# Layer 2's scans joined into one product, and pool waits narrowed to the bytes that are reused, in a four-layer image network

## The chip, the cores and the metric

The kernel runs on one core of one Trainium2 chip. The metric is the device time in microseconds of one execution. The kernel before takes 7064.17 us (median of 3 runs, 7053.81 to 7065.25); the profiled execution spans 7063.8 us. Everything is float32.

The engines are named as in the profile: PE is TensorE (matrix products; PEld is its loading of weights, which overlaps the products), DVE is VectorE, ACT is ScalarE, POOL is GpSimd, SP is the engine whose queue starts most DMA transfers. SBUF is the on-chip memory with 128 partitions, PSUM the smaller one in which TensorE leaves its results, and DRAM the memory outside.

## The reference

Four residual layers on x of shape 8 x 56 x 56 x 192. Each one is `x = x + layer(groupnorm(x))`:

```python
x = x + _L0(_gn(x))   # gated Toeplitz mixing along rows and columns
x = x + _L1(_gn(x))   # attention in shifted 7 x 7 windows
x = x + _L2(_gn(x))   # 3 x 3 convolution and running averages
x = x + _L3(_gn(x))   # 7 x 7 convolution, LayerNorm, wide MLP with gelu
```

The part that is rewritten lies in layer 2. It projects to 384 channels, convolves each channel, and adds running averages in four directions:

```python
def ema_scan(x, axis):                 # s = 0.6 s + 0.4 x, along one axis
    ...
proj  = jnp.einsum('bhwd,dc->bhwc', x, W_in) + b_in
local = depthwise_conv_3x3(proj)       # cut: the call
lr = ema_scan(local, 3)                # left to right
rl = flip(ema_scan(flip(local, 3), 3), 3)
tb = ema_scan(local, 2)                # top to bottom
bt = flip(ema_scan(flip(local, 2), 2), 2)
mixed = 0.25 * (lr + rl + tb + bt) + local
# then LayerNorm over the channels and W_out
```

## The kernel before

The program works through nine stages, one after the other: `qv` (layer 0, projections), `mix` (layer 0, Toeplitz products), `l1` (layer 1), `l2i`, `mx`, `l2o` (layer 2: in, mixing, out), `l3i`, `cv`, `l3o` (layer 3: in, convolution, out). Each stage opens pools of its own for SBUF and PSUM and closes them at its end; between stages the images pass through DRAM (`x1`, `x2`, `pd`, `md`, `xd`, `zd`, `yd`). A new stage's pools use the bytes of the pools that were closed:

```python
    with ExitStack() as st:
        pool = st.enter_context(tc.tile_pool(name="l2i", bufs=2))
        psum = st.enter_context(tc.tile_pool(name="l2ip", bufs=4, space=PSUM))
        w_in = resident("w_in", nc.gpsimd, pool)
        b_in = resident("b_in", nc.gpsimd, pool)
        for b in range(nimg):
            layer2_in(b, pool, psum, w_in, b_in)
    layer2_mix()
    with ExitStack() as st:
        pool = st.enter_context(tc.tile_pool(name="l2o", bufs=2))
        # ... and so on for every stage
```

Without any other word, a pool's first users wait until everything of the pool that it replaces is done. `bufs=2` gives each name in the pool two buffers. The tiles lie in the order in which their names are first used. The order of instructions in each engine's queue is fixed when the program is built; it follows the program's text, except that an instruction that is expected to be ready sooner may go ahead of one that is not.

Layer 2's mixing works on 24 groups of 16 channels, all 8 images at once. A column of 128 partitions holds two neighbouring rows of an image: row 0 of the pair on the upper 64 partitions, row 1 on the lower 64, the 56 pixels of a row reversed. `NPAIR` is 28 pairs of rows, `NG` is 8 x 28 = 224 columns of one channel. Running top to bottom over rows is then a scan over pairs with the factor 0.6 x 0.6 = 0.36, and the left and right averages within a row are part of the matrix `ema`:

```python
            for g in range(C2 // CG2):
                cs = slice(g * CG2, (g + 1) * CG2)
                wt = pool.tile([128, CG2, 256], F32, name="wt2")
                nc.sync.dma_start(wt, ...)                      # band matrices of 16 channels
                zc = pool.tile([128, nimg, CG2, P2], F32, name="zc2")
                for b in range(nimg):
                    nc.sync.dma_start(zc[:, b], pd[b][:, cs])
                loc = pool.tile([128, CG2, NG], F32, name="loc")
                fwd = pool.tile([128, CG2, NG], F32, name="fwd")
                bwd = pool.tile([128, CG2, NG], F32, name="bwd")
                for c4 in range(0, CG2, 4):
                    ps = psum.tile([128, 2, 512], F32, name="cv2")
                    for i in range(4):
                        dst = ...
                        for q in range(2):
                            nc.tensor.matmul(                   # the convolution
                                dst, wt[:, c4 + i, 128 * q:128 * q + 128], zc[:, :, c4 + i, q:q + NPAIR],
                                start=(q == 0), stop=(q == 1),
                            )
                    nc.scalar.copy(
                        loc[:, c4:c4 + 4].rearrange("p (j i) z -> p j (i z)", j=2), ps[:, :, 0:2 * NG]
                    )
                for h in range(2):
                    ...
                    nc.vector.tensor_tensor_scan(f(fwd), d, f(loc), 0.0, ALU.mult, ALU.add)
                    nc.vector.tensor_tensor_scan(
                        _reversed(f(bwd)), d, _reversed(f(loc)), 0.0, ALU.mult, ALU.add
                    )
                yc = pool.tile([2 * W, nimg, CG2, NPAIR], F32, name="yc2")
                for c4 in range(0, CG2, 4):
                    ps = psum.tile([2 * W, 2, 512], F32, name="mx2")
                    for i in range(2):
                        for k, z in enumerate((loc, fwd, bwd)):
                            nc.tensor.matmul(                   # three products, summed in PSUM
                                ps[:, i, 0:2 * NG], ema[:, k],
                                z[:, c4 + 2 * i:c4 + 2 * i + 2].rearrange("p c z -> p (c z)"),
                                start=(k == 0), stop=(k == 2),
                            )
                    for i in range(2):                          # src, dst: cut
                        if i == 0:
                            nc.vector.tensor_copy(dst, src)
                        else:
                            nc.scalar.copy(dst, src)
                for b in range(nimg):
                    nc.sync.dma_start(md[b][:, cs], yc[:, b])
```

A float32 product of this program appears in the trace as two matmul instructions.

Of the kernel before, what the change touches and what calls it, by code (L numbers as in the profile page):

```python
# [76 lines left out]
def kernel(ctx: ExitStack, tc: tile.TileContext, a: dict, out: bass.AP):  # L77
# [208 lines left out]


    def build_bias_mask(psum):
        with tc.tile_pool(name="bm", bufs=2) as pool:
            rev = pool.tile([WN, WN], F32, name="rev", bufs=1)  # L290
            nc.gpsimd.dma_start(rev, a["rev49"])

# [482 lines left out]
    def layer2_mix():  # L775

        band = a["band2"]
        with ExitStack() as st:  # L780
            pool = st.enter_context(tc.tile_pool(name="mx", bufs=2))
            psum = st.enter_context(tc.tile_pool(name="mxp", bufs=2, space=PSUM))
            ema = resident("ema", nc.gpsimd, pool)
            NG = nimg * NPAIR
            dec = pool.tile([128, CG2 * nimg, NPAIR], F32, name="dec2", bufs=1)
            nc.gpsimd.memset(dec, 0.36)
            nc.gpsimd.memset(dec[:, :, 0:1], 0.0)
            dec = dec.rearrange("p c n -> p (c n)")
            for g in range(C2 // CG2):
                cs = slice(g * CG2, (g + 1) * CG2)  # L790
                wt = pool.tile([128, CG2, 256], F32, name="wt2")
                nc.sync.dma_start(
                    wt, bass.AP(band.tensor, band.offset + g * CG2 * BL2, [[1, 128], [BL2, CG2], [1, 256]])
                )
                zc = pool.tile([128, nimg, CG2, P2], F32, name="zc2")
                for b in range(nimg):
                    nc.sync.dma_start(zc[:, b], pd[b][:, cs])
                loc = pool.tile([128, CG2, NG], F32, name="loc")
                fwd = pool.tile([128, CG2, NG], F32, name="fwd")
                bwd = pool.tile([128, CG2, NG], F32, name="bwd")  # L800
                for c4 in range(0, CG2, 4):
                    ps = psum.tile([128, 2, 512], F32, name="cv2")
                    for i in range(4):
                        dst = ps[:, i // 2, NG * (i % 2):NG * (i % 2 + 1)].rearrange("p (b n) -> p b n", n=NPAIR)
                        for q in range(2):
                            nc.tensor.matmul(  # L806
                                dst, wt[:, c4 + i, 128 * q:128 * q + 128], zc[:, :, c4 + i, q:q + NPAIR],
                                start=(q == 0), stop=(q == 1),
                            )
                    nc.scalar.copy(  # L810
                        loc[:, c4:c4 + 4].rearrange("p (j i) z -> p j (i z)", j=2), ps[:, :, 0:2 * NG]
                    )
                for h in range(2):
                    hs = slice(h * CG2 // 2, (h + 1) * CG2 // 2)
                    f = lambda z: z[:, hs].rearrange("p c z -> p (c z)")
                    d = dec[:, 0:CG2 // 2 * NG]
                    nc.vector.tensor_tensor_scan(f(fwd), d, f(loc), 0.0, ALU.mult, ALU.add)  # L817
                    nc.vector.tensor_tensor_scan(
                        _reversed(f(bwd)), d, _reversed(f(loc)), 0.0, ALU.mult, ALU.add
                    )  # L820
                yc = pool.tile([2 * W, nimg, CG2, NPAIR], F32, name="yc2")
                for c4 in range(0, CG2, 4):
                    ps = psum.tile([2 * W, 2, 512], F32, name="mx2")
                    for i in range(2):
                        for k, z in enumerate((loc, fwd, bwd)):
                            nc.tensor.matmul(  # L826
                                ps[:, i, 0:2 * NG], ema[:, k],
                                z[:, c4 + 2 * i:c4 + 2 * i + 2].rearrange("p c z -> p (c z)"),
                                start=(k == 0), stop=(k == 2),
                            )  # L830
                    for i in range(2):
                        src = ps[:, i, 0:2 * NG].rearrange("p (c b n) -> p b c n", c=2, n=NPAIR)
                        dst = yc[:, :, c4 + 2 * i:c4 + 2 * i + 2]
                        if i == 0:
                            nc.vector.tensor_copy(dst, src)
                        else:
                            nc.scalar.copy(dst, src)
                for b in range(nimg):
                    nc.sync.dma_start(md[b][:, cs], yc[:, b])

    def layer2_out(b, pool, psum, w_out):

# [76 lines left out]
    def convolve():  # L919

        band = a["band"]
        with ExitStack() as st:
            pool = st.enter_context(tc.tile_pool(name="cv", bufs=2))
            psum = st.enter_context(tc.tile_pool(name="cvp", bufs=3, space=PSUM))
            for g in range(C // CG):
                cs = slice(g * CG, g * CG + CG)
                wt = pool.tile([OP, CG, BAND], F32, name="wt")
# [95 lines left out]

    scsh = const.tile([128, nimg, 2, 3], F32, name="scsh")
    with ExitStack() as st:
        pool = st.enter_context(tc.tile_pool(name="qv", bufs=2))
        psum = st.enter_context(tc.tile_pool(name="qvp", bufs=4, space=PSUM))
        w_qv = resident("w_qv", nc.scalar, pool)
        b_qv = pool.tile([2 * W, 2, D1], F32, name="b_qv", bufs=1)
        nc.scalar.dma_start(b_qv.rearrange("p a d -> p (a d)"), a["b_qv"].partition_broadcast(2 * W))  # L1030
        tz = st.enter_context(tc.tile_pool(name="tz", bufs=2))
        x = layer0_load(0, pool)
        xn = layer0_in(0, x, pool, psum)
        blocks = toeplitz_rows(psum, tz)
        build_bias_mask(psum)
        for b in range(nimg):

            between = {i: blocks.pop(0) for i in (1, 7, 12) if blocks}
            ahead = []
            if b + 1 < nimg:  # L1040
                x = layer0_load(b + 1, pool)
                between[4] = lambda: ahead.append(layer0_in(b + 1, x, pool, psum))
            layer0_qv(b, xn, pool, psum, w_qv, b_qv, between)
            xn = ahead[0] if ahead else None
        for block in blocks:
            block()
    with ExitStack() as st:
        pool = st.enter_context(tc.tile_pool(name="mix", bufs=2))
        psum = st.enter_context(tc.tile_pool(name="mixp", bufs=2, space=PSUM))
        w_p = resident("w_p", nc.gpsimd, pool)  # L1050
        w_o = resident("w_o", nc.gpsimd, pool)

        ops = [psum.tile([128, 8, H], F32, name=f"op{k}", bufs=1) for k in range(2)]
        for op in ops:
            nc.vector.memset(op, 0.0)
        layer0_mix(pool, psum, ops, w_p, w_o)


    with ExitStack() as st:
        pool = st.enter_context(tc.tile_pool(name="l1", bufs=2))  # L1060
        psum = st.enter_context(tc.tile_pool(name="l1p", bufs=1, space=PSUM))
        consts = layer1_weights(pool, psum)

        ones2 = pool.tile([128, 128], F32, name="ones2", bufs=1)
# [46 lines left out]


    with ExitStack() as st:
        pool = st.enter_context(tc.tile_pool(name="l2i", bufs=2))
        psum = st.enter_context(tc.tile_pool(name="l2ip", bufs=4, space=PSUM))
        w_in = resident("w_in", nc.gpsimd, pool)
        b_in = resident("b_in", nc.gpsimd, pool)
        for b in range(nimg):
            layer2_in(b, pool, psum, w_in, b_in)
    layer2_mix()  # L1120
    with ExitStack() as st:
        pool = st.enter_context(tc.tile_pool(name="l2o", bufs=2))
        psum = st.enter_context(tc.tile_pool(name="l2op", bufs=2, space=PSUM))
        w_out = resident("w_out", nc.gpsimd, pool)
        for b in range(nimg):
            layer2_out(b, pool, psum, w_out)
    with ExitStack() as st:
        pool = st.enter_context(tc.tile_pool(name="l3i", bufs=2))
        psum = st.enter_context(tc.tile_pool(name="l3ip", bufs=2, space=PSUM))
        gmat = resident("gmat", nc.gpsimd, pool)  # L1130
        for b in range(nimg):
            layer3_in(b, pool, psum)


    convolve()
    with tc.tile_pool(name="l3o", bufs=2) as pool, tc.tile_pool(name="l3op", bufs=2, space=PSUM) as psum:
        w0 = resident("w0", nc.gpsimd, pool)
        w1 = resident("w1", nc.gpsimd, pool)
        dwb = pool.tile([OP, C], F32, name="dwb", bufs=1)
# [6 lines left out]
def _lay_out(inp):  # L1146
# [37 lines left out]
        band2[:, 126 + 64 * i:129 + 64 * i] = l2("conv_w")[:, 0, i]  # L1184
    at = 127 - (64 * np.arange(2)[:, None] + np.arange(W))
    eye, near = np.eye(W), 0.6 ** np.abs(np.arange(W)[:, None] - np.arange(W))
    ema = np.zeros((128, 3, 2, W))
    for r in range(2):
        for s in range(2):
            back = 0.6 ** (s - r)  # L1190
            ema[at[r], 0, s] = (1.1 * eye + 0.1 * near) if r == s else -eye / 6.0
            ema[at[r], 1, s] = 0.1 * back * eye
            ema[at[r], 2, s] = 0.1 / back * eye

    b_in = np.zeros((2, 64, 3, 2, C2), np.float32)
    b_in[:, 0:W] = l2("b_in")
# [25 lines left out]
        "w_qkv": twice(l1("w_qkv")), "w_proj": halves(l1("w_proj")), "sel": sel,  # L1222
        "rel": l1("rel_table")[::-1].T, "mask": l1("mask_matrix"),
        "w_in": twice(l2("W_in")), "b_in": b_in.reshape(128, 3, 2, C2), "band2": band2,
        "ema": ema.reshape(128, 3, 2 * W).astype(np.float32), "w_out": blocks(l2("W_out")),
        "w0": twice(l3("w0")), "w1": blocks(l3("w1")),
    }.items()}

# [17 lines left out]
```

## Time and profile before

| what | us or share |
|---|---|
| time, median of 3 | 7064.17 |
| TensorE busy | 6002.1 (85%) |
| VectorE busy | 3210.2 (45%) |
| ScalarE busy | 1811.4 (26%) |
| GpSimd busy | 1039.3 (15%) |
| DRAM traffic | 147 GB/s over the span |
| share of TensorE in the chain that ended last | 60% |
| stretch of layer 2's mixing stage | 4225 to 5050 |

The profile is one execution. A line of a group of instructions gives the source line, the engine, the operation, the tile written and the tiles read, the shapes, how many, the busy time and mean duration, and at the end the idle time of the engine before them with what ended it. A stretch gives, between two times, how long each engine was busy (with the number of instructions), the clock that TensorE was granted as a share of full speed, the share of time that the DMA engines were busy, and what they moved. Matrix products overlap in the pipeline, so their mean duration is more than the time from one to the next. A busy share over the whole span hides that stages have different limits, so the stages are looked at one by one.

### The profile page before, as it was taken

To read this page: it belongs to the slowest core of one execution; us is meant where nothing else is said; L and a number is where in the kernel's file an instruction comes from. 1 tells how busy PE (TensorE), PEld (TensorE's weight loads), DVE (VectorE), ACT (ScalarE), POOL (GpSimd) and SP (SyncE) were. 2 spreads that over 40 slices of the span, in tenths; PEclk is the share of its full clock that TensorE was granted. 3 is DMA by queue.
4 is the path that set the end of the run, shared out by engine and by line. 5 is a ranking of instruction groups with operands and counts; after the bars stand their busy time and mean duration, and the time that the engine had idled before them with its cause. 6 is when DMAs were issued, how large, how long until landed. Compare 5 with 4: busy or idle time off the path is not lost.

```text
span 7063.8 us, 126329 instructions
## 1 busy us (share of the span) xinstructions
PE 6002.1 (85%) x56258; PEld 3967.7 (56%) x56258; DVE 3210.2 (45%) x4598; ACT 1811.4 (26%) x2528; POOL 1039.3 (15%) x564
## 2 busy tenths in 40 slices
PE   6789989999999688888885878999688569698999
PEld 5568767777777344544553445666434369444444
DVE  6677733333333344444443764555477521423231
ACT  2234421111111233333331001111255100133333
POOL 4200033333333011211221000000000000101000
PEclk8889989999999788888886889999888579799999
DMA  8998886555554524444424545455577679412120
GB/s 196 210 199 173 166 287 231 222 216 216 216 216 171 77 41 57 57 56 58 57 43 76 171 157 200 165 171 174 143 170 167 182 260 325 138 50 78 52 64 25
DMA packets 1045489, 1047.05 MB, mean 148 GB/s; under 512 B 831340, under 2 KB 963860, under 8 KB 1017424
## 3 DMA queue, kind: packets, MB, share of 16 engines
q1 hardware_dynamic: 1031776, 973.57, 49.9%
q0 software_dynamic: 11440, 62.42, 3.5%
q8 instruction: 441, 7.23, 0.4%
q10 hardware_dynamic: 1728, 2.99, 0.1%
q14 instruction: 104, 0.85, 0.0%
HBM read 693.71 MB, written 345.07 MB: 147 GB/s over the span
## 4 chain that ended last, share of the span: by engine, by line
PE 60%; DVE 14%; DMA 9%; issue 6%; ACT 4%; SPq 3%; POOL 3%; DVEq 0%; another core or an unknown queue 0%; POOLq 0%; ACTq 0%
PE op L404 7%; PE qv L348 6%; PE po L1009 5%; PE pj L426 5%; PE y L447 5%; PE ph L1000 5%; PE qk_ps L627 3%; PE cps L940 3%; PE mx L826 3%; DVE ln_st L207 3%; PE cv L806 3%; PE pr L729 2%; DMA x<-x 2%; DVE fwd L817 2%; PE po L870 2%
## 5 line engine op out<-in xcount | busy, mean ns | idle before, releaser
L348 PE MATMUL qv<-w_qv_sb,xn 64*112 64x288 f32 x5376 | 733.3, 427 | 104.2 <-DVE act L354 104.2
L348 PEld LDWEIGHTS qv<-w_qv_sb,xn 64*112 64x112 f32 x5376 | 560.9, 184 | 273.8 <-DVE act L354 130.6
L385 POOL COPY lc<-lt 128x1792 f32<-128x1792 f32 x144 | 474.2, 3295 | 834.2 <-PE op L404 745.7
L404 PE MATMUL op<-rt,lc 128*56 128x56 f32 x9216 | 561.6, 275 | 3.2 <-DMA rt<-right 2.9
L404 PEld LDWEIGHTS op<-rt,lc 128*56 128x56 f32 x9216 | 507.7, 145 | 75.7 <-issue 58.8
L1009 PE MATMUL po<-hid,w_sb 128*64 128x392 f32 x2304 | 399.8, 506 | 64.7 <-ACT hid L1004 64.7
L1000 PE MATMUL ph<-y,w_sb 64*128 64x392 f32 x2304 | 423.8, 501 | 10.4 <-ACT hid L1004 10.4
L355 ACT ACTIVATE act<-act 112x576 f32<-112x576 f32 x448 | 301.1, 683 | 500.5 <-DVE act L354 499.9
L426 PE MATMUL pj<-xn,w_p_sb 64*128 64x392 f32 (+1 forms) x1920 | 372.8, 510 | 27.6 <-DVE xn L468 23.1
L447 PE MATMUL y<-pp,w_o_sb 128*64 128x392 f32 (+1 forms) x1920 | 353.1, 499 | 1.6 <-DVE pp L440 1.2
L1016 DVE TENSOR_TENSOR x<-x,z 128x392 f32<-128x392 f32 x96 | 54.5, 568 | 646.7 <-ACT z L1014 646.7
L440 DVE TENSOR_TENSOR pp<-pp,ot 128x784 f32<-128x784 f32 (+1 forms) x160 | 155.1, 969 | 404.6 <-ACT pp L431 396.8
L354 DVE TENSOR_TENSOR act<-qv,b_qv 112x576 f32<-112x576 f32 x448 | 317.2, 749 | 37.7 <-PE qv L348 37.7
L1000 PEld LDWEIGHTS ph<-y,w_sb 64*128 64x128 f32 x2304 | 233.1, 189 | 175.9 <-issue 26.7
L1009 PEld LDWEIGHTS po<-hid,w_sb 128*64 128x64 f32 x2304 | 165.3, 140 | 295.8 <-issue 225.1
L806 PE MATMUL cv<-zc,wt 128*128 128x224 f32 x1536 | 301.7, 355 | 29.8 <-DMA zc<-pd 29.8
L940 PE MATMUL cps<-zc,wt 128*128 128x224 f32 x1536 | 299.4, 356 | 30.4 <-DMA zc<-zd 28.8
L627 PE MATMUL qk_ps<-xr,wg 64*96 64x392 f32 x1536 | 311.4, 514 | 13.8 <-ACT qk L633 10.5
L806 PEld LDWEIGHTS cv<-zc,wt 128*128 128x128 f32 x1536 | 290.6, 189 | 46.2 <-issue 39.2
L940 PEld LDWEIGHTS cps<-zc,wt 128*128 128x128 f32 x1536 | 289.7, 189 | 40.0 <-issue 32.6
L764 PE MATMUL pin<-w_in_sb,xn 64*128 64x384 f32 x1392 | 259.9, 520 | 57.2 <-POOL xn L755 38.2
L431 ACT ACTIVATE pp<-pj,vecs_sb 128x784 f32<-128x784 f32 (+1 forms) x160 | 146.3, 915 | 571.3 <-PE pj L426 569.1
(220 smaller groups left out, 8873.1 us busy)
## 6 DMA issues: line engine op xcount, KB each, us to landing
lt<-left SPq DMA_DIRECT2D x72, 1792.0 KB
rt<-right SPq DMA_DIRECT2D x72, 1792.0 KB
left<-qv SPq DMA_DIRECT2D x224, 252.0 KB
right<-qv SPq DMA_DIRECT2D x448, 126.0 KB
wt<-in_band_dram SPq DMA_DIRECT2D x24, 2048.0 KB
wt<-in_band_dram SPq DMA_DIRECT2D x12, 4096.0 KB
pd<-pt SPq DMA_DIRECT2D x8, 5568.0 KB
zc<-pd SPq DMA_DIRECT2D x192, 232.0 KB
```

The source lines that it names most:

```text
L348: nc.tensor.matmul(ps[s][:, which, 0:D1 // 2], xn[64 * s:64 * s + 64, j, bass.ts(i, 2 * W)], w_qv[64 * s:64 * s + 64, j, which, ns], start ...
L354: nc.vector.tensor_tensor(act, ps[s][:, :, 0:D1 // 2], b_qv[:, :, ns], ALU.add)
L355: nc.scalar.activation(act, act, AF.Silu)
L385: nc.gpsimd.tensor_copy(lc.rearrange("p (u d) w -> p u d w", u=nu), raw[0].rearrange("p (w u d) -> p u d w", u=nu, d=64 // nu)[:, :, nh * ...
L404: nc.tensor.matmul(op[64 * u:64 * u + W, i, :], lc[:, nh * u + d0 + i], rc[:, u, d0 + i], start=True, stop=True)
L426: nc.tensor.matmul(ps[0:M, s, 0:TT], w_p[64 * s:64 * s + 64, j, d0:d0 + M], xn[64 * s:64 * s + 64, j, ts], start=(j == 0), stop=(j == 2),)
L447: nc.tensor.matmul(y[64 * s:64 * s + 64], w_o[0:M, c, 64 * j:64 * j + 64], pp[0:M, s], start=(c == gated[0][0]), stop=(c == gated[-1][0]),)
L627: nc.tensor.matmul(ps[s], wg[64 * s:64 * s + 64, j, c0:c0 + HC], xw[64 * s:64 * s + 64, j, gs], start=(j == 0), stop=(j == 2),)
L806: nc.tensor.matmul(dst, wt[:, c4 + i, 128 * q:128 * q + 128], zc[:, :, c4 + i, q:q + NPAIR], start=(q == 0), stop=(q == 1),)
L940: nc.tensor.matmul(dst.rearrange("p (b n) -> p b n", n=NPAIR), wt[:, c4 + i, q * OP:(q + 1) * OP], zc[:, :, c4 + i, q:q + NPAIR], start=(q ...
L1000: nc.tensor.matmul(ps[:, s, 0:TT], w0[64 * s:64 * s + 64, j, m * 128:(m + 1) * 128], y[64 * s:64 * s + 64, j, ts], start=(j == 0), stop=(j ...
L1009: nc.tensor.matmul(ps[64 * s:64 * s + 64], w1[:, m, 64 * j:64 * j + 64], hid[:, m, s], start=(m == 0), stop=(m == 5),)
```

## The change

There are two parts.

**Waits of reused bytes.** Every stage's pools, with the one that prepares the masks, get `reuse_waits="tile"`. A tile in such a pool waits only for the users of the bytes on which it comes to lie, where before it waited for all users of the pools that were there. This is to let a stage's first loads begin while the stage before is still at work. Data that passes through DRAM is waited for as before.

```diff
-        pool = st.enter_context(tc.tile_pool(name="l2i", bufs=2))
-        psum = st.enter_context(tc.tile_pool(name="l2ip", bufs=4, space=PSUM))
+        pool = st.enter_context(tc.tile_pool(reuse_waits="tile", name="l2i", bufs=2))
+        psum = st.enter_context(tc.tile_pool(reuse_waits="tile", name="l2ip", bufs=4, space=PSUM))
         # ... the same in qv, tz, bm, mix, l1, mx, l2o, l3i, cv, l3o
```

**Layer 2's averages.** The sum that a pair of rows brings to a scan is formed before the scan: ScalarE writes the other row of the pair, times 1/0.6, onto the same partitions, and GpSimd adds the row itself. Then one tile `sums` holds a forward scan on its upper 64 partitions and a backward scan on its lower 64, and one product with `ema[:, 1]` replaces the two of before. The loop is also staggered: `back` of one group (products, copies out) alternates with `front` of the next (convolution, row sums, scans), four channels at a time.

```diff
+            def front(c4, wt, zc, loc, rows, sums):
+                ps = psum.tile([128, 2, 512], F32, name="cv2")
+                ...                                   # the convolution, as before
+                nc.scalar.copy(pair(loc), ps[:, :, 0:2 * NG])
+                for r in range(2):
+                    nc.scalar.activation(
+                        pair(rows)[64 * r:64 * r + 64], ps[64 - 64 * r:128 - 64 * r, :, 0:2 * NG], AF.Identity,
+                        scale=1.0 / 0.6,
+                    )
+                nc.gpsimd.tensor_tensor(rows, rows, loc, ALU.add)
+                d = dec[:, 0:4 * NG]
+                nc.vector.tensor_tensor_scan(sums[64:128], d[64:128], rows[64:128], 0.0, ALU.mult, ALU.add)
+                nc.vector.tensor_tensor_scan(
+                    _reversed(sums[0:64]), d[0:64], _reversed(rows[0:64]), 0.0, ALU.mult, ALU.add
+                )
+
+            def back(c4, yc, loc, rows, sums):
+                ps = psum.tile([2 * W, 2, 512], F32, name="mx2")
+                for i in range(2):
+                    for k, z in enumerate((loc, sums)):
+                        nc.tensor.matmul(..., ema[:, k], ..., start=(k == 0), stop=(k == 1))
+                ...                                   # copies to yc, as before
-                for h in range(2):
-                    ...
-                    nc.vector.tensor_tensor_scan(f(fwd), d, f(loc), 0.0, ALU.mult, ALU.add)
-                    nc.vector.tensor_tensor_scan(
-                        _reversed(f(bwd)), d, _reversed(f(loc)), 0.0, ALU.mult, ALU.add
-                    )
-                        for k, z in enumerate((loc, fwd, bwd)):
+            loaded, now, n = [load(0)], None, C2 // CG2
+            for g in range(n + 1):
+                if g + 1 < n:
+                    loaded.append(load(g + 1))
+                yc = pool.tile([2 * W, nimg, CG2, NPAIR], F32, name="yc2") if g else None
+                following = [pool.tile([128, CG2, NG], F32, name=z) for z in ("loc", "rows", "sums")] if g < n else None
                 for c4 in range(0, CG2, 4):
+                    if g:
+                        back(c4, yc, *now)
+                    if g < n:
+                        front(c4, *loaded[g], *following)
+                if g:
+                    for b in range(nimg):
+                        nc.sync.dma_start(md[b][:, (g - 1) * CG2:g * CG2], yc[:, b])
+                now = following
...
-    ema = np.zeros((128, 3, 2, W))
+    ema = np.zeros((128, 2, 2, W))
...
-            ema[at[r], 1, s] = 0.1 * back * eye
-            ema[at[r], 2, s] = 0.1 / back * eye
+            ema[at[r], 1, s] = 0.1 * 0.6 ** (1 - s if r else s) * eye
```

## The prediction

> **What bounds the kernel now.** I read the page first: TensorE is busy 85% of the span, the next engine (VectorE) 45%, and the chain that ended last is 60% TensorE. So time can come back in two ways: less TensorE work where TensorE is the limit, or less waiting where TensorE is empty. The change touches both, so I cut the span into stages (busy time by stretch) and looked at layer 2's mixing stage and at the seams between stages. Layer 2's mixing stage, and one of its 24 channel groups in steady state (columns: stretch, length, PE, PEld, DVE, ACT, POOL busy, granted clock, DMA share, GB/s):
>
> ```profile
> 4225.00:5050.00 825.00, 743.32 (x2689) 490.45 (x2688) 421.68 (x193) 137.02 (x192) 3.97 (x3) 0.98 0.50 170
> ...
> 4586.30:4619.10 32.80, 30.55 (x112) 20.06 (x111) 17.24 (x9) 5.66 (x8) 0.00 (x0) 1.00 0.50 171
> ```
>
> A group takes 32.8 us and TensorE is busy 30.6 of it, at full clock. GpSimd is idle, ScalarE nearly so, DMA half busy. The groups of instructions in this stage:
>
> ```profile
> L806 PE MATMUL cv<-zc,wt 128*128 128x224 f32 x1536 | 301.7, 355 | 29.8 <-DMA zc<-pd 29.8
> L817 DVE TENSOR_TENSOR_SCAN fwd<-dec,loc 128x1792 f32<-128x1792 f32 x48 | 186.2, 3879 | 187.4 <-ACT loc L810 187.4
> L826 PE MATMUL mx<-bwd,ema_sb 128*112 128x448 f32 x384 | 177.8, 545 | 25.2 <-DVE bwd L818 25.2
> L826 PE MATMUL mx<-loc,ema_sb 128*112 128x448 f32 x384 | 177.8, 545 | 22.2 <-ACT yc L837 22.2
> L810 ACT COPY loc<-cv 128x896 f32<-128x896 f32 x96 | 87.0, 906 | 270.9 <-PE cv L806 199.4 <-DMA zc<-pd 71.5
> ```
>
> There are 64 convolution instructions a group (1536/24) and 48 mixing ones (3 x 384/24: local part, forward, backward). The means of 355 and 545 ns overlap in the pipeline; the pace is read from the chain in order of time, where 64 cv instructions take 12.32 us (0.193 each), and from the timeline, where mx instructions follow each other every 0.376 us. 12.3 + 48 x 0.376 = 30.4 us: that is the 30.6 above. The other 2.2 us are two waits a group (25.2 + 22.2 us in all, about 1 us each): the products need the backward scan, then an emptied PSUM buffer, because VectorE runs the second half's scans before its copies.
>
> The seams. Each stretch below runs from the last product of a stage to the first steady products of the next (same columns):
>
> ```profile
> 926.50:959.70 33.20, 9.06 (x32) 4.21 (x28) 6.67 (x11) 2.45 (x4) 7.34 (x4) 0.59 0.92 322
> 2320.50:2420.00 99.50, 42.40 (x134) 22.63 (x135) 28.18 (x46) 16.89 (x22) 7.64 (x15) 0.61 0.91 120
> 3805.60:3876.20 70.60, 6.57 (x28) 6.26 (x28) 11.97 (x28) 1.58 (x2) 4.21 (x9) 0.53 0.92 126
> 4225.50:4255.00 29.50, 0.00 (x0) 0.01 (x1) 0.64 (x1) 0.00 (x0) 3.97 (x3) 0.56 0.90 348
> 5046.00:5102.80 56.80, 0.00 (x0) 0.00 (x0) 23.50 (x39) 1.65 (x3) 0.54 (x1) 0.52 0.96 232
> 5511.00:5551.70 40.70, 0.93 (x4) 0.79 (x4) 11.75 (x27) 0.26 (x1) 3.08 (x8) 0.56 0.80 179
> 5716.20:5744.00 27.80, 0.14 (x2) 0.08 (x1) 0.76 (x1) 0.50 (x1) 0.00 (x0) 0.50 0.90 349
> 6046.00:6101.80 55.80, 0.09 (x2) 0.06 (x1) 23.18 (x40) 0.85 (x2) 22.21 (x11) 0.52 0.86 252
> ```
>
> They add up to 414 us with TensorE busy for 59: store the last image, wait until it has landed, then begin the next stage's loads.
>
> [...] In layer 3's output stage three tiny VectorE additions, 0.20 us elsewhere, last as long as the GpSimd addition beside them (timelines of the two engines):
>
> ```profile
> 6088.85 10.30 POOL L963 TENSOR_TENSOR yl<-yl,dwb 128x1344 f32<-128x1344 f32 x4 [2.42 <-DMA yl<-yd]
> ...
> 6091.38 2.70 DVE L212 TENSOR_TENSOR ln_d<-ln_st 128x28 f32<-128x28 f32 x1
> 6094.00 2.72 DVE L215 TENSOR_TENSOR ln_var<-ln_st 128x28 f32<-128x28 f32 x1
> 6096.65 2.55 DVE L213 TENSOR_TENSOR ln_d<-ln_d 128x28 f32<-128x28 f32 x1
> ```
>
> [...] Here VectorE's copies from PSUM of 448 and 768 elements take 0.62 and 0.96 us, so about 0.15 us is fixed; small beside a scan. [...]
>
> **The change part by part.** *Products.* Forward and backward scans go into one tile: 32 mixing instructions a group instead of 48. Removed: 16 x 0.376 = 6.0 us of the engine that bounds the stage. New TensorE work: 12.3 + 32 x 0.376 = 24.35 us a group.
>
> *Order.* The products of group g-1 now alternate, four channels at a time, with the convolution of group g. Products then read scans finished about a group earlier, so the wait for the backward scan (1 us) should go. A step of four channels is 3.1 + 3.0 = 6.1 us of TensorE. Against that:
> - VectorE: eight scans of 896 elements on 64 partitions instead of four of 1792 on 128. Lane for lane the same 7168 elements: 0.15 + 3.73/2 = 2.0 us each, 4.0 a step, plus a 0.62 copy: 4.6 of 6.1.
> - ScalarE: per step a 0.91 copy, two new activations of 896 from PSUM (0.9 to 1.0 each, from the 0.91), a 0.53 copy: about 3.4.
> - GpSimd: one addition of 896: its 1176-element additions take 2.19 us (two groups of layer 1), so 1.67.
> - [...] The addition waits for ScalarE and the scans wait for the addition, so they alternate anyway[...].
> - DMA: a group moves 2048 KB of weights, 8 x 232 in and 8 x 196 KB out, 5.6 MB, at 32.8 us 171 GB/s. At 25 us it is 224 GB/s; layer 3's convolution sustains 323.
>
> I take 25.0 us a group, 0.65 over the TensorE sum. 24 x 32.8 = 787 becomes 24 x 25.0 + 5 for the last chain = 605: **182 us saved**, all on the path since TensorE bounds the stage.
>
> *Reuse waits.* A tile no longer waits for the whole earlier pool. What it gains is set by which bytes the first tiles land on (I laid the pools out in order of first use from their sizes) and by true data dependences through DRAM, which stay. Estimates from the timelines:
> - 926 to 960: the first lt can come early, x and rt land on weights and on the last image; 8.
> - 2320: the first x1 lands on image 7's x (bytes 41-60K over 30-48K), still to be stored; then 60 us of normalisation chain. 5.
> - 3806: loads begin at 3839, after a 33 us store of small pieces. Image 0's x2 lands on the masks' and exponentials' bytes, free near 3797; landing 18 us later, TensorE would start near 3835 instead of 3876. The load must be queued ahead of the store; 35.
> - 4225: weights and seven images of zc come early; the last store (15 us) and a 232 KB piece stay. 10.
> - 5046: ml needs the last store; less beside it. 8.
> - 5511: x3i overlaps w_out, so it starts at the last product rather than after the 13 us store. 13.
> - 5716: 4 MB of weights from 5707, beside the store. 12.
> - 6046: yl lands partly on the last weights; loads of w0, w1 and dwb leave its way. 15.
>
> Sum **106 us** of 414. Total: 7064 - 182 - 106 = 6776, rounded to **6775**.
>
> **Rivals.** *A serial ring takes the stage.* If the queues of VectorE and ScalarE held strict program order, ScalarE's yc copy would stand behind VectorE's (its waits name "DVE yc L835" in this stage), that behind the scans, those behind the addition and ScalarE's own row sums: 0.91 + 1.9 + 1.7 + 4.0 + 0.62 + 0.53 + hand-overs = 10 us a step, 40 a group: 173 us lost instead of 182 saved, net about 7130. Against it: the timeline shows queues reordered by readiness (loads of group 1 issued ahead of group 0's stores; transposes and po products interleaved in layer 2's output). A milder form, VectorE and GpSimd blocking each other so that a step takes 6.6, costs 1.4 us a group, 34 us: near 6810.
>
> *The transfer is hidden by another transfer.* DMA is at 0.80 to 0.96 in all eight seams, so early loads may only share bandwidth with the store they overlap. If seams give 40 us, the time is about 6840. For it: seams at 4225 and 5716 already run near 350 GB/s. Against it: those at 2320, 3806 and 5511 move only 120 to 180.
>
> *Better placement than mine.* If more first tiles land on idle bytes, the seams could give 170: 6710.
>
> **Range and chances.** Mixing saves 140 to 195 and the seams 40 to 165, mostly independent: 6700 to 6890 as the range. Faster by over 2% means under 6923; only the ring, or a failure in both parts, prevents it: 0.92, within 2% 0.06, slower 0.02.
>
> **What would show it.** In the changed profile: 768 mx instructions instead of 1152; a group of 24.5 to 25.5 us with TensorE over 95% busy; scans near 2.0 us, the GpSimd addition near 1.7, both lengthened if they block each other; loads of a stage issued before the last store of the one before; the 3806 seam some 35 us shorter, the 2320 one nearly as it was. I am wrong if TensorE waits for yc or for sums in every step, if the scans on 64 partitions are slower per element, or if loads placed early hold up stores behind them in the queue.

## The result, and the profile after

| | before | after |
|---|---|---|
| median, us | 7064.7 (7053.8 to 7070.5) | 6846.9 (6839.1 to 6855.7) |
| ratio to before, 95% interval | 1 | 0.9694 (0.9675 to 0.9712) |
| span of the profile, us | 7063.8 | 6850.9 |
| layer 2's mixing stage, first convolution to last product, us | 790 | 607 |
| one channel group in it, us | 32.80 | 24.73 |
| the eight seams, us | 414 | 373 |

218 us were saved where 289 had been predicted. The mixing stage gave 183 us, the predicted 182 to within one. The seams gave 41 instead of 106. (The two profiled executions differ by 213 us. 183 + 41 is 224, so the other stages together took some 11 us longer; layers 0 and 1 alone, whose work is the same, took 16 more.)

One group of the mixing stage after the change, by stretch (columns: stretch, length, PE, PEld, DVE, ACT, POOL busy, granted clock, DMA share, GB/s):

```profile
4500.00:4524.73 24.73, 24.73 (x98) 17.53 (x97) 21.82 (x13) 12.65 (x16) 9.39 (x5) 1.00 0.68 227
```

The view shows no gap of TensorE, at full clock. The groups of instructions of the same stage of the changed kernel (busy us and mean ns of one, then the idle time before them and what ended it):

```profile
L824 DVE TENSOR_TENSOR_SCAN sums<-dec,rows 64x896 f32<-64x896 f32 x96 | 280.0, 2917 | 1.3
L821 POOL TENSOR_TENSOR rows<-rows,loc 128x896 f32<-128x896 f32 x96 | 228.5, 2380 | 391.1 <-ACT rows L817 263.7 <-issue 127.3
L823 DVE TENSOR_TENSOR_SCAN sums<-dec,rows 64x896 f32<-64x896 f32 x96 | 195.7, 2039 | 104.7 <-POOL rows L821 103.1
L832 PE MATMUL mx<-loc,ema_sb 128*112 128x448 f32 x384 | 181.3, 554 | 5.9 <-ACT yc L843 5.9
L832 PE MATMUL mx<-sums,ema_sb 128*112 128x448 f32 x384 | 176.6, 542 | 2.0 <-DVE sums L824 2.0
```

There are 768 mixing products instead of 1152, and the two waits of before (25.2 and 22.2 us) have become 2.0 and 5.9. The two scans of a step do equal work and yet take 2.04 and 2.92 us; that is taken up below.

The eight seams after the change, same columns as for the group, in the order of the prediction's list:

```profile
931.50:960.10 28.60, 6.47 (x24) 3.00 (x22) 6.20 (x9) 2.26 (x3) 5.17 (x4) 0.64 1.00 339
2322.50:2414.60 92.10, 37.95 (x130) 20.28 (x130) 27.15 (x45) 16.88 (x22) 6.88 (x14) 0.65 0.97 120
3809.80:3876.60 66.80, 6.64 (x29) 6.27 (x28) 11.96 (x28) 0.30 (x1) 3.61 (x8) 0.53 0.90 124
4223.10:4251.70 28.60, 0.00 (x0) 0.00 (x0) 0.84 (x1) 0.00 (x0) 3.97 (x3) 0.56 0.98 365
4858.70:4915.60 56.90, 0.00 (x0) 0.00 (x0) 23.77 (x39) 1.66 (x3) 0.57 (x1) 0.52 1.00 237
5324.00:5363.60 39.60, 0.96 (x4) 0.79 (x4) 11.76 (x27) 0.26 (x1) 3.18 (x8) 0.56 0.80 184
5528.20:5555.10 26.90, 0.00 (x0) 0.02 (x1) 0.64 (x1) 0.50 (x1) 0.00 (x0) 0.50 0.97 359
5856.00:5889.30 33.30, 0.14 (x1) 0.01 (x1) 14.81 (x40) 0.85 (x2) 10.31 (x4) 0.53 0.95 302
```

| seam into | before | after | gained | predicted |
|---|---|---|---|---|
| layer 0's mixing | 33.2 | 28.6 | 4.6 | 8 |
| layer 1 | 99.5 | 92.1 | 7.4 | 5 |
| layer 2's input | 70.6 | 66.8 | 3.8 | 35 |
| layer 2's mixing | 29.5 | 28.6 | 0.9 | 10 |
| layer 2's output | 56.8 | 56.9 | -0.1 | 8 |
| layer 3's input | 40.7 | 39.6 | 1.1 | 13 |
| layer 3's convolution | 27.8 | 26.9 | 0.9 | 12 |
| layer 3's output | 55.8 | 33.3 | 22.5 | 15 |

One seam gave over half of it. Two timelines of the changed kernel say why that one did and the largest miss did not. First GpSimd at layer 3's output (start, length, what):

```profile
5831.63 1.07 POOL L96 DMA_DIRECT2D w_sb<-in_w_dram  x2 [325.96 <-PE cps L961]
...
5871.98 10.31 POOL L984 TENSOR_TENSOR yl<-yl,dwb 128x1344 f32<-128x1344 f32 x4 [38.73 <-DMA yl<-yd]
```

The weights are issued 24 us before the stage before has ended. GpSimd's queue, from which they come, had nothing else in it. The addition waits for its data, yl, and no longer for the bias vector dwb, and begins 16 us after the last product instead of 30 us. VectorE's three small additions, which before lasted as long as GpSimd's beside them (2.55 to 2.72 us), now come after those and take 0.20 us each. Now SyncE's queue and GpSimd at layer 2's input (last product of layer 1 ends near 3809.8):

```profile
3807.92 36.90 SPq L562 DMA_DIRECT2D x<-x  x18
3844.99 0.59 SPq L744 DMA_DIRECT2D x<-x  x1
```

```profile
3811.34 0.26 POOL L741 MEMSET x<- 64x168 f32 x1
```

GpSimd clears the border rows of image 0's tile (L741) at 3811. Its bytes are free, as the prediction said. But the load (L744) is issued at 3845, 0.2 us after the last of 18 stores of the stage before (L562). It waits for no buffer. It stands behind them in one queue. In the built program no engine has any instruction of a later stage ahead of one of an earlier stage.

### The profile page after: what moved, and what is told of

The parts are those of the page before. It is cut to its first block, busy times and chain, and to the rows that moved or that the text cites. A ratio compares the mean times of both kernels' runs of the same rounds, so it can differ in the third digit from the quotient of the medians.

```text
span 6850.9 us, 126015 instructions
## 1 busy us (share of the span) xinstructions
PE 5860.9 (86%) x55874; PEld 3905.1 (57%) x55874; DVE 3308.6 (48%) x4694; ACT 1978.1 (29%) x2720; POOL 1268.0 (19%) x660
## 4 chain that ended last, share of the span: by engine, by line
PE 58%; DVE 13%; DMA 9%; issue 8%; ACT 5%; POOL 4%; SPq 3%; DVEq 0%; POOLq 0%; ACTq 0%
PE op L404 8%; PE qv L348 7%; PE po L1030 5%; PE pj L426 5%; PE y L447 5%; PE ph L1021 5%; PE cps L961 4%; PE qk_ps L627 4%; PE pr L729 3%; DVE ln_st L207 3%; DMA right<-qv 2%; DMA x<-x 2%; PE po L891 2%; PE v_ps L647 2%; PE ot L437 2%
## 5 line engine op out<-in xcount | busy, mean ns | idle before, releaser
L808 PE MATMUL cv<-zc,wt 128*128 128x224 f32 x1536 | 313.4, 356 | 28.6 <-DMA zc<-pd 28.6
L677 POOL TENSOR_TENSOR e<-e,mx 128x1176 f32<-128x1176 f32 x64 | 140.0, 2188 | 957.5 <-DVE mx L676 836.1
```

The source lines that it names most:

```text
L808: nc.tensor.matmul(dst, wt[:, c4 + i, 128 * q:128 * q + 128], zc[:, :, c4 + i, q:q + NPAIR], start=(q == 0), stop=(q == 1),)
```

## The experiments

Layers 0 and 1 do the same work in all kernels of this section, and yet their last product comes anywhere between 3791 and 3836 us in the profiles. So effects on a stage are read inside it, from its first to its last instruction. Times of kernels are given as ratio to the kernel before on the same chip.

### The two parts alone

**Mixing alone**: the new loop, with the waits of before.

```diff
-        pool = st.enter_context(tc.tile_pool(reuse_waits="tile", name="mx", bufs=2))   # and the 19 others alike
+        pool = st.enter_context(tc.tile_pool(name="mx", bufs=2))
```

> The new mixing loop with the old pool waits. If the two parts simply add: before minus the mixing stage's gain in the changed kernel (790 to 607 us between first convolution product and last mixing product, 183 us), so 6880 us, between 6870 and 6890; the seams stay as before (the last one near 56 us). Rival: the staggered loop needs the narrowed waits to start its loads early; then the stage is longer than 607 us and the time over 6895.

Ratio 0.9734 (0.9721 to 0.9747), 6901.4 us: 185 us saved. The stage lasts 605 us. (The expected 6880 counts from 7064; on this chip the kernel before took 7086.7, and 183 less is 6904.)

**Waits alone**: the old loop with `reuse_waits="tile"` in every pool.

> The old mixing loop with the narrowed pool waits. If the parts add: 7064 - 34 = 7030 us, with 22 us of it from the last seam (to layer 3's output stage) and 1 to 8 us from each other. Rival: the narrowed waits were worth more and part of it was hidden or lost beside the new loop; then under 7010 us.

Ratio 0.9943 (0.9930 to 0.9955), 7049.3 us: 37 us saved. The two ratios multiply to 0.968, within the interval of the whole change. At this precision no influence of one part on the other is seen, and each can be judged alone: the loop gives what was predicted, the waits about a third of what was.

### The mixing stage: which of its two ideas pays

**Staggered order, three products.** The sums stay the old ones (a forward and a backward scan over 128 partitions each, no row sums, no addition on GpSimd), in steps of four channels; only the order is new.

```diff
-                for r in range(2): nc.scalar.activation(pair(rows)[...], ps[...], AF.Identity, scale=1.0 / 0.6)
-                nc.gpsimd.tensor_tensor(rows, rows, loc, ALU.add)
+                nc.vector.tensor_tensor_scan(rows, d, loc, 0.0, ALU.mult, ALU.add)
+                nc.vector.tensor_tensor_scan(_reversed(sums), d, _reversed(loc), 0.0, ALU.mult, ALU.add)
...
-                    for k, z in enumerate((loc, sums)):
+                    for k, z in enumerate((loc, rows, sums)):
```

> The changed kernel with the old sums: the staggered loop, but forward and backward scans of 128 partitions in two tiles, no row sums, and three products again. If the fewer products are what was gained and the order only removes two waits a group: 12.3 + 18.0 = 30.4 us of TensorE, 30.4 to 31.0 us a group, and 24 x 5.9 = 142 us slower than the changed kernel (ratio to before near 0.989). Rival: the order brought most of it; then under 28 us a group.

Ratio 0.9857 (0.9831 to 0.9883), 6968.0 us. One of its groups, by stretch:

```profile
4501.46:4531.74 30.28, 30.28 (x113) 20.52 (x112) 17.76 (x13) 5.75 (x8) 0.00 (x0) 1.00 0.56 185
```

TensorE is full with the work that the prediction had worked out (30.4). The stage lasts 730 us, 60 less than before, and 123 more than in the changed kernel (142 were expected).

**One product, old order**: all convolutions of a group, then all its products.

```diff
-                for c4 in range(0, CG2, 4):
-                    if g: back(c4, yc, *now)
-                    if g < n: front(c4, *loaded[g], *following)
+                for c4 in range(0, CG2, 4): front(c4, *loaded, *now)
+                for c4 in range(0, CG2, 4): back(c4, yc, *now)
```

> The changed kernel with one product for both scans but each group's convolution ahead of its own products, as before. If the order is only worth the two waits: 24.4 + 2 to 4 us, so 26.4 to 28.4 a group, 40 to 90 us slower than the changed kernel. Rival: without the order the row sums, addition and scans of the last four channels (about 9 us) lie open in every group: 30 us or more a group, and the new sums alone bring under 70 us.

Ratio 1.0005 (0.9997 to 1.0014), 7069.7 us. The stage lasts 836 us, 46 more than before with a third of the mixing products gone; what the narrowed waits give elsewhere only pays that back. The whole stage as a stretch, and a line of its groups of instructions:

```profile
4248.90:5084.80 835.90, 675.41 (x2304) 436.69 (x2304) 563.31 (x288) 312.32 (x383) 299.80 (x96) 0.90 0.46 154
```

```profile
L832 PE MATMUL mx<-sums,ema_sb 128*112 128x448 f32 x384 | 219.7, 659 | 122.1 <-DVE sums L824 122.1
```

Here TensorE waits for the sums, 122 us in all (and 38 us more for emptied buffers), and its products take longer: 659 ns a product against 542 in the changed kernel, with a granted clock of 0.90 over the stage against 0.99 there. So the stage lost more than its waits: TensorE is busy 675 us in it, where 24 groups at the prediction's TensorE sum of 24.35 us, which is for full clock, are 584. The loads of a group are no longer issued a group ahead here, but only the first product of the stage waits for one. The new sums need a longer chain than the old: ScalarE's row sums, GpSimd's addition, two scans. The staggered order gives that chain a whole group of time. The order alone is worth 60 us, the new sums within it 123 (730 to 607), and the new sums without it minus 46.

The same kernel shows most clearly that GpSimd's additions and VectorE's scans last longer side by side. GpSimd's timeline, then VectorE's:

```profile
4500.94 10.55 POOL L821 TENSOR_TENSOR rows<-rows,loc 128x896 f32<-128x896 f32 x3 [0.89 <-ACT rows L817]
```

```profile
4502.12 3.74 DVE L824 TENSOR_TENSOR_SCAN sums<-dec,rows 64x896 f32<-64x896 f32 x1
...
4513.39 2.02 DVE L823 TENSOR_TENSOR_SCAN sums<-dec,rows 64x896 f32<-64x896 f32 x1
```

Alone an addition takes 2.08 us and a scan 2.02. Side by side they take 3.5 and 3.7: each is longer by most of the other's length (1.4 and 1.7 us).

**The same, addition on VectorE.**

```diff
-                nc.gpsimd.tensor_tensor(rows, rows, loc, ALU.add)
+                nc.vector.tensor_tensor(rows, rows, loc, ALU.add)
```

Two reasons why the old order is as slow as it is were weighed: that additions and scans lengthen each other, as in the timelines above (3.5 and 3.7 us), and the length of the chain behind the last convolution.

> Old order (all convolutions of a group, then all its products), new sums, with the addition on VectorE instead of GpSimd; compared with the same order with the addition on GpSimd (7069.7 us, 34.7 us a group from the first convolution to the last product). [...] the four pairs of scans then take 4 x 5.0 on VectorE and the group some 29 to 31 us, so 80 to 120 us shorter (about 6950 to 6990). 'The length of the chain behind the last convolution does, whoever adds': one addition is 1.1 us shorter and one scan 0.9 us, the group 33 us or more, at most 45 us shorter (7025 or more).

Ratio 0.9901 (0.9885 to 0.9918), 7001.3 us: 68 less, between the two expectations. The stage is 766 us, 70 less, and 24 less than before. Both scans are 2.02 us now and the addition 1.07. TensorE now hardly waits for the sums (1.9 us between 4260 and 4840), but for an emptied PSUM buffer (84.2 us). So in the old order the addition on GpSimd costs 70 us; in the staggered order, by the next run, it costs 20. And the order is worth 229 us with the addition on GpSimd (836 to 607), 179 with it on VectorE (766 to 587). The two effects don't simply add. The 70 are not divided further: the edit takes away the longer scans (2.45 and 2.88 us on average against 2.02) and a slower addition (2.08 against 1.07) at once.

**The changed kernel, addition on VectorE.** The same one-line edit in the staggered loop.

> The addition of the two rows moves from GpSimd to VectorE, nothing else. VectorE's work in a step is then about 1.0 (896 sums) + 4.04 (two scans at 2.02) + 0.55 (yc) = 5.6 us, under TensorE's 6.09. 'GpSimd and VectorE get in each other's way and set the pace': the backward scan's mean falls from 2.92 us to about 2.02, the group from 24.73 to 24.35-24.5 us, and the kernel is 6 to 12 us shorter than the changed one (about 6837, ratio to the kernel before .968). 'TensorE alone sets the pace': scans shorter, group still 24.7, no gain. 'The chain on VectorE becomes too long': group over 25 us and the kernel over 10 us longer than the changed one.

Ratio 0.9671 (0.9657 to 0.9686), 6839.8 us. One group by stretch, and its backward scan and addition in the groups of instructions between 4260 and 4840:

```profile
4500.00:4524.34 24.34, 24.34 (x97) 17.70 (x97) 22.67 (x17) 13.05 (x16) 0.00 (x0) 1.00 0.71 231
```

```profile
L824 DVE TENSOR_TENSOR_SCAN sums<-dec,rows 64x896 f32<-64x896 f32 x94 | 189.6, 2017 | 1.3
...
L821 DVE TENSOR_TENSOR rows<-rows,loc 128x896 f32<-128x896 f32 x95 | 103.2, 1087 | 64.1 <-ACT rows L817 64.1
```

Both scans take 2.02 us now. The group falls to 24.34 us, the TensorE sum of the prediction (24.35) itself, and the stage from 607 to 587: 9 us from 24 groups at 0.39, the other 11 at the start and the end of the stage, where the changed kernel's first and last products wait for sums and for an emptied buffer. So a busy share of 100% had hidden a small wait: the ends of products are modelled, and fill short gaps. The period of the groups shows the wait, and so do the loads of weights. Who waited for whom in the changed kernel between 4300 and 4840, in us in all, times and longest:

```profile
PEld mx L832 <- ACT yc L843: 12.9, 44, 0.4
```

Twice a group TensorE waited for ScalarE's copy of yc to empty a PSUM buffer; with the addition on VectorE the same view has no such line. By the kernels' ratios the gain over the changed kernel (0.9694) is not certain, as the intervals overlap; the stage's 20 us is read from the profiles.

### The seams: queue, bytes or bandwidth

**Loads from ScalarE's queue.** Layer 2's first two images and the mixing stage's first group are loaded from another queue than the stores.

```diff
+        eng = nc.scalar if b < 2 else nc.sync
-        nc.sync.dma_start(x[0:64, :, 1:R2], src[:, :, 0:R2 - 1])
+        eng.dma_start(x[0:64, :, 1:R2], src[:, :, 0:R2 - 1])
...
+                eng = nc.scalar if g == 0 else nc.sync      # wt and zc of the mixing stage
```

> The changed kernel with the first two image loads of layer 2's input stage and the first group's loads of its mixing stage issued from ScalarE's queue, which has nothing left to do in the stage before, instead of SyncE's. Theory 'queue order' (each queue holds a whole stage before any of the next, so a load waits behind the last stores in the same queue): the loads of layer 2's input start near 3811 instead of 3845 and TensorE some 15 to 25 us earlier; the mixing loads start near 4192 instead of 4224 and its first product comes 8 to 10 us earlier: 6847 - 28 = 6819 us (6812 to 6828). Theory 'bandwidth' (the loads only share the transfer engines with the stores): same time as the changed kernel within 6 us. Theory 'bytes' (the tiles land on bytes in use to the end): the loads still start at 3840 or later, same time.

Ratio 0.9673 (0.9658 to 0.9687), 6859.1 us. The seam into the mixing stage went from 28.6 to 22.6 us: weights issued 36 us before the last product of the stage before, and still the data are the last to come. The seam into layer 2's input gained nothing:

```profile
3873.28 0.66 ACTq L745 DMA_DIRECT2D x<-x  x1
```

The stores in this run occupy SyncE's queue from 3834.5 to 3872.9; the load comes 0.4 us after, although it is in another queue. It is not the bytes: GpSimd clears the border of the same tile at 3838. It is not the order within one queue alone either; what held the load until 3873 is not shown.

**Loads from GpSimd's queue.** The same edit with `nc.gpsimd`, for layer 2's first two images only.

> The changed kernel with layer 2's first two image loads issued from GpSimd's queue. From ScalarE's queue they still started after the last store[...]. [...] the loads start within 5 us of the last product, during the stores, and the seam of 66 us falls by 10 to 25 us. Theory 'bytes': they start after the stores again (30 us or more after the last product), seam 64 us or more. Theory 'bandwidth': they start early but land no sooner, because the stores' small pieces keep the transfer engines at 0.9: seam 60 us or more.

Ratio 0.9661 (0.9637 to 0.9684), 6828.8 us. GpSimd's timeline, SyncE's and TensorE's:

```profile
3801.09 0.64 POOL L745 DMA_DIRECT2D x<-x  x1
```

```profile
3796.87 58.36 SPq L562 DMA_DIRECT2D x<-x  x18
```

```profile
3839.12 16.11 PE L765 MATMUL pin<-w_in_sb,xn 64*128 64x384 f32 x84 [4.61 <-POOL xn L756]
3874.20 4.04 PE L765 MATMUL pin<-w_in_sb,xn 64*128 64x384 f32 x12 [18.96 <-DVE pt L773]
```

The load goes out 4 us after the first store and the seam is 40.3 us instead of 66.8: the predicted gain exists, it is 26 of the 35 us. But the same 18 stores now take 58 us instead of 37, with the loads running beside them; image 2's load, issued from SyncE's queue, waits behind them until 3855; VectorE stands in its queue at that image's statistics (20.6 us) with image 0's bias additions behind them, and TensorE waits for those (19 us). From the last product of layer 1 to the first of the mixing stage it is 436 us against 442: 6 of the 26 are kept in this profile.

**Layer 3's input off the last weights' bytes.** 2560 unused bytes per partition move x3i away from w_out.

```diff
+        pool.tile([128, 640], F32, name="pad", bufs=1)
         gmat = resident("gmat", nc.gpsimd, pool)
```

> The changed kernel with 2560 unused bytes ahead of layer 3's first input tile, so that the tile no longer lies on layer 2's output weights, which are in use to the last product. Theory 'bytes': its load and statistics start before the last product, the seam of 40 us shrinks by 13 us or more, 6834 us or less. Theory 'queue order': the load still stands behind the last store in SyncE's queue, so the seam stays at 38 to 40 us and the time at 6847, within 5 us.

Ratio 0.9682 (0.9669 to 0.9695), 6865.8 us. The seam is 39.7 us, as before the move. Other tiles of the stage are cleared 22 us before the last product, so bytes are free, and the load still follows the last stores. Free bytes alone give nothing.

**The same, image 0 from ScalarE's queue.**

```diff
-        nc.sync.dma_start(x, xd[b].rearrange("(k p) n -> p k n", p=HC))
+        (nc.scalar if b == 0 else nc.sync).dma_start(x, xd[b].rearrange("(k p) n -> p k n", p=HC))
```

> As moved_only, and image 0's load of layer 3's input stage is issued from ScalarE's queue, whose last work of the stage before ends about 19 us ahead of the last product. Theory 'queue order': the load is issued near 19 us before the last product instead of 2 us after it, and the seam between last product and first transposed pixels falls from 40 us to between 10 and 20. Theory 'bytes' or 'bandwidth': the seam stays at 36 us or more.

Ratio 0.9675 (0.9651 to 0.9699), 6835.6 us. Issued 19 us before the last product, the load has landed by the time VectorE is free; and yet the seam is 32 us, not 10 to 20. ScalarE's timeline and VectorE's (last product at 5326.7):

```profile
5307.78 0.34 ACTq L906 DMA_DIRECT2D x3i<-xd  x1
```

```profile
5331.74 3.31 DVE L144 BATCH_NORM_STATS2 gn_st<-x3i 96x6 f32<-96x392 f32 x7
5351.36 0.56 DVE L144 BATCH_NORM_STATS2 gn_st<-x3i 96x6 f32<-96x392 f32 x1 [16.32 <-DMA x3i<-xd]
```

All statistics of image 0 are made by 5335. The next in VectorE's order is one statistic of image 1, whose load is still behind the stores; image 0's final aggregate stands behind it and waits 16 us. Once more an order within a queue, now VectorE's.

### Together

The addition on VectorE; all of layer 2's image loads from GpSimd's queue; the mixing stage's first loads from ScalarE's; x3i moved, its first *two* images from ScalarE's queue. The changed kernel ran beside it.

> The changed kernel itself, beside the next one on one chip: 6835 to 6860 us, ratio .967 to .970.

> What the single steps showed, put together in the changed kernel: the addition on VectorE; every image's first load of layer 2 from GpSimd's queue; the mixing stage's first loads from ScalarE's queue; layer 3's input off w_out's bytes and its first two images' loads from ScalarE's queue. 'Seams are orders of queues': mixing stage 20 us shorter (24.34 a group), the seam to layer 2 25 us or more and, with image 2's load no longer behind the stores, most of it kept over the stage (15 to 25), the seam to the mixing stage 4 to 6, the seam to layer 3's input 13 to 20: 50 to 70 us below the changed kernel. 'Each load that comes forward takes its time from another transfer': not more than the sum of what the single runs kept, 8 + 6 + 2 + 12 = 28 us.

The changed kernel: 6854.1 us, 0.9676 (0.9663 to 0.9689). Together: 6833.0 us, 0.9648 (0.9635 to 0.9662), the lowest ratio of these runs (its interval overlaps those of several of them), but 21 us below the changed kernel and not the 50 hoped for. The number is that of the second expectation, at most 28. Two of its seams, into layer 2's input and layer 3's input, by stretch (the DMA share of 1.07 is as the view gives it):

```profile
3822.80:3863.10 40.30, 6.58 (x28) 6.27 (x28) 11.98 (x28) 0.30 (x1) 5.32 (x11) 0.55 1.07 177
...
5340.70:5354.10 13.40, 0.99 (x5) 0.85 (x5) 11.73 (x27) 0.26 (x1) 0.00 (x0) 0.69 0.95 232
```

| stretch, us (starts of products) | changed kernel | together |
|---|---|---|
| seam into layer 2's input | 71.0 | 40.8 |
| layer 2's input, first to last product | 345.7 | 399.8 |
| seam into the mixing stage | 29.1 | 22.5 |
| mixing stage | 606 | 587 |
| layer 2's output, with the seam into it | 463.5 | 467.5 |
| seam into layer 3's input | 40.2 | 13.9 |

With image 1's load early as well, the seam into layer 3's input is 13.9 us: nothing but the normalisation chain, and the 16 us wait is gone. That bears out what held the run before. The loss is layer 2's input, 54 us longer, and it came from my edit: a load stood behind what lay ahead of it in its queue here too, now GpSimd's. Its timeline:

```profile
3885.78 0.70 POOL L750 MEMSET xn<- 128x720 f32 x1 [22.16 <-DMA x<-x]
...
3887.17 0.63 POOL L744 DMA_DIRECT2D x<-x  x1
```

Image 2's load (L744) stands behind a clearing of image 1's xn, which waits until the stores have left its bytes; image 3's stands behind one that waits 35 us for TensorE. In image 0 TensorE waits 25 us for bias additions that stand in VectorE's queue behind statistics of a late load, and in each of images 1 to 5 once 3 to 4 us; in all it waits 53 us for such additions, against 20 in the changed kernel. A version with only the first images on GpSimd's queue and the rest as here was not run.

## Why the prediction was right, and where it was not

**Right: the size of the mixing stage, from the TensorE sum.** 25.0 us a group were predicted, 24.73 measured; TensorE above 95%, 100%; scans "near 2.0", 2.02; ScalarE's row sums 0.9 to 1.0, 0.91. Neither the serial ring nor its mild form at 6.6 us a step came: a step takes 6.18. That the stage's 183 us meet the predicted 182 so closely is partly luck: the groups are 0.27 us shorter than predicted (6 to 7 us in all), and the start and end of the stage cost some 13 us where 5 were allowed.

**Mis-sized within it: the GpSimd addition, "so 1.67".** It was scaled from an addition in layer 1 and takes 2.08 us undisturbed, 2.38 on average beside the scans. The argument "they alternate anyway" is wrong: an addition of the next step often falls on a backward scan, which then takes 3.8 us (2.92 on average). The addition on GpSimd costs little (0.39 us a group and 11 us at the stage's ends, by the run with it on VectorE), as the products read sums a group old.

**Mis-sized: "the wait for the backward scan (1 us) should go".** The order removes both waits, 2.5 us a group (32.80 to 30.3), 60 us of the 183; the predicted 25.0 us a group left 1.8 for it beside the 6.0 of the product. The prediction listed these 6.0 us as a gain of their own. They are not: without the order the new sums cost 46 us, and with the addition on VectorE they brought 24.

**Wrong: the seams, 106 predicted, 41 measured.** The failed step is "The load must be queued ahead of the store; 35". I named the condition and then counted it as met, because "the timeline shows queues reordered by readiness". That reordering exists within a stage; across stages none was built. A narrower wait lets a tile be used earlier, but the instruction that would use it stands behind the last stores of the stage before. This is why the seam into layer 2's input gained 3.8 us instead of 35. The timelines show the same for those into layer 3's input and convolution, 1 each instead of 13 and 12: their first loads are issued right after the last stores, at 5326.1 and 5529.5. The seam that gained most, 22.5 for a predicted 15, is the one whose weights come from a queue with nothing in front of them. The total stayed in the predicted range because the stage gave most of it; 41 us lie at the edge of the 40 to 165 allowed for the seams.

**The rival "the transfer is hidden by another transfer"** had the right total (40 us, "about 6840") with another cause than the one that acted: in the changed kernel the first image loads of layers 2 and 3 were issued after the stores and not beside them. Where an experiment issued them so, the rival showed itself: stores at 58 us instead of 37, and 20 of 26 us given back. How much of that is shared bandwidth, and how much is what waited behind the stores, was not separated.

**Left open.** What held the load in ScalarE's queue until 0.4 us after the stores was not shown; in GpSimd's queue the load went out 4 us after the first store. Why the seams into layer 0's mixing, layer 1 and layer 2's output gained 4.6, 7.4 and -0.1 us was not examined.

## What to carry to other kernels

When a wait on a buffer is narrowed, look next at the queue of the instruction that was waiting: in these runs the freed time was had only where nothing slower stood in front of it, and this went for the queue of transfers (a load issued 0.2 us after the last of 18 stores) and for the orders of VectorE and GpSimd alike (16 and 22 us of waiting). A reformulation that trades work of the bounding engine for a longer chain elsewhere may need a staggered loop, so that the chain has an iteration to run in: the same sums lost 46 us here without it and brought 123 with it. Test the two apart. And measure TensorE at 100% by the period of its loop, not by its busy share.

## What the runs showed of the hardware

- A scan of 896 elements takes 2.02 us on 64 or on 128 partitions, one of 1792 on 128 takes 3.87: the time went by elements per partition.
- The same fp32 addition of 896 elements takes 2.08 us on GpSimd and 1.07 to 1.09 on VectorE, and GpSimd beside a scan costs both (3.5 and 3.7 us).
- In the seam with eighteen stores in small pieces (21433 of the 22329 packets there are under 512 bytes) the DMA engines are at a share of 0.90 while it moves 124 GB/s; three other seams move 339 to 365 GB/s at 0.97 to 1.00. With loads issued beside them, these stores took 58 us instead of 37.
